# Last node stage of a two-layer graph network: batch norm, elu and residual with feature columns on the partitions

## The chip, the cores and the metric

The kernel runs on one core of a Trainium2 chip. The metric is device time in microseconds of one launch; lower is better. One profiled execution of the kernel before stands beside three timed runs.

## The reference, cut to what matters

There are N = 6250 nodes with D = 256 features, and E = 100000 edges sorted by destination. The first layer is a typed graph attention layer; the second is a graph attention layer with 4 heads of 64 columns. Each layer is preceded by a layer norm and a relu and followed by a residual. Only the end of the second layer is touched by the change:

```python
out = jax.ops.segment_sum(msg, dst, num_segments=n)   # softmax-weighted messages, per node and head
h = out.reshape(n, H * C) + bias
mu = jnp.mean(h, axis=0)                              # over the 6250 nodes, one per column
var = jnp.var(h, axis=0)
h = (h - mu) * jax.lax.rsqrt(var + BN_EPS) * gamma + beta
h = jax.nn.elu(h)
return feature + h                                    # and the outer residual: x + that
```

The mean and the variance run over the nodes, so three passes over the nodes are needed: one that builds h, one that sums squared differences, one that scales.

## The kernel before, in words

The kernel has several stages one after another: sorting of edges, the typed projections, the two edge loops (each a long software pipeline of gathers, matmuls and accumulations), and between and behind them stages over nodes. Each stage with a data-dependent tail ends with branches that all engines take, so nothing of the last stage starts before the edge loop ahead of it has ended.

The last stage (L1797 to L1872) holds nodes on the partitions. A block is 127 nodes on partitions 1 to 127 (partition 0 carries nothing real), and there are NB = 50 blocks, the last of 27 nodes. `acc1` holds for each block, head and node the 64 weighted sums, the denominator and the weight of the node's own message (its self loop). `xw_d` in DRAM holds the projected features (260 numbers per node), `r_d` what the residual adds (256 per node).

Its steps, which the prediction calls A to E:

- Step A, build. Per block two loads (`load_rows`, L173: 112 and 15 rows), then four VectorE operations of 256 columns: own features times own weight (L1832), plus accumulated messages (L1833), times reciprocal denominator (L1834), plus bias (L1835), into `hg`, which keeps all blocks in SBUF. A matmul with a mask of real rows (L1836) adds each block into `sum_ps`.
- Step B, the mean: one ScalarE copy from PSUM (L1838).
- Step C, variance. In ten groups of five blocks: VectorE subtracts the mean in place (L1842), ScalarE squares (L1844), TensorE sums over the rows with five masked matmuls (L1847).
- Step D, scale: Sqrt on ScalarE (L1849), reciprocal and product with gamma on VectorE, on tiles of 128x256 (L1850, L1851).
- Step E, normalise, elu, residual. In ten groups: VectorE multiplies by the scale (L1861), adds beta (L1862), takes the minimum with 0 (L1864), ScalarE takes Exp (L1865), VectorE subtracts 1 (L1866), takes the maximum and adds (L1867), and adds the residual (L1868) that was loaded from `r_d` into one of two buffers (L1858, L1860). The result is stored (L1870, L1872).

All loads and stores of the stage are issued by SyncE in order, through one hardware queue. The order on each engine is set by a scheduler that interleaves the written loops; each engine then works its list strictly in order. TensorE's matmuls of f32 operands show as two weight loads and two matmuls each in the trace, its transposes as one of each.

Two earlier lines serve the prediction as rows to measure by: L410, a VectorE operation with two inputs in SBUF, and L441, a GpSimd multiply of 64x384 with one broadcast input, which runs beside it early in the kernel. L1409 and L1385 are GpSimd additions of 128x256 in the node stage of the first layer, L490 a GpSimd copy of 128x1024, L325 ScalarE operations of 128x896 that also give a sum along the row, L1407 a ScalarE operation with a bias and a scale per partition.

Of the kernel before, what the change touches and what calls it, by code (L numbers as in the profile page):

```python
# [24 lines left out]
def kernel(  # L25
# [1771 lines left out]
    with ExitStack() as st:  # L1797
        cst = st.enter_context(tc.tile_pool(name="e1c", bufs=1))
        wk = st.enter_context(tc.tile_pool(name="e1w", bufs=3))
        pp = st.enter_context(tc.tile_pool(name="e1p", bufs=1, space=PSUM))  # L1800
        rowc = cst.tile([P, 3, D], F32, name="rowc")
        for i, a in enumerate((g_bias, gamma, beta)):
            nc.scalar.dma_start(rowc[:, i, :], bcast(a, D))
        GB = 5
        assert NB % GB == 0
        XB = 4
        xbuf = cst.tile([P, XB, H * XW], F32, name="xbuf")
        nc.gpsimd.memset(xbuf, 0.0)

        real = cst.tile([P, 2, P], F32, name="real")  # L1810
        for i, n in enumerate((BN, LAST)):
            inside = cst.tile([P, 2], F32, name="inside%d" % i)
            nc.vector.tensor_scalar(inside[:, 0:1], ipart, 1.0, None, op0=OP.is_ge)
            nc.vector.tensor_scalar(inside[:, 1:2], ipart, float(n), None, op0=OP.is_le)
            nc.vector.tensor_scalar(real[:, i, :], ones, inside[:, 0:1], inside[:, 1:2], op0=OP.mult, op1=OP.mult)
        xbuf = xbuf.rearrange("p x (h e) -> p x h e", h=H)
        hg = cst.tile([P, NB, D], F32, name="hg")
        es = cst.tile([P, NB, H], F32, name="es")
        den = cst.tile([P, NB, H], F32, name="den")
        for o, i in ((den, DK), (es, DK + 1)):  # L1820
            nc.vector.tensor_tensor(
                o, acc1[:, :, :, i], nhas[:, :, None].to_broadcast([P, NB, H]), op=OP.add
            )
        nc.vector.reciprocal(den, den)
        rbuf = cst.tile([P, 2, GB, D], F32, name="rbuf")
        nc.gpsimd.memset(rbuf, 0.0)
        sum_ps = pp.tile([P, D], F32, name="sum_ps")
        for b in range(NB):
            xs = xbuf[:, b % XB]
            load_rows(xs.rearrange("p h e -> p (h e)"), xw_d, b)  # L1830
            xw = wk.tile([P, H, DK], F32, name="xw")
            nc.vector.tensor_tensor(xw, xs[:, :, :DK], es[:, b, :, None].to_broadcast([P, H, DK]), op=OP.mult)  # L1832
            nc.vector.tensor_add(xw, xw, acc1[:, b, :, :DK])  # L1833
            nc.vector.tensor_tensor(xw, xw, den[:, b, :, None].to_broadcast([P, H, DK]), op=OP.mult)  # L1834
            nc.vector.tensor_add(hg[:, b, :], xw.rearrange("p h e -> p (h e)"), rowc[:, 0, :])  # L1835
            nc.tensor.matmul(sum_ps, real[:, b == NB - 1, :], hg[:, b, :], start=(b == 0), stop=(b == NB - 1))  # L1836
        mu = cst.tile([P, D], F32, name="mu")
        nc.scalar.activation(mu, sum_ps, AF.Copy, scale=1.0 / N)  # L1838
        var_ps = pp.tile([P, D], F32, name="var_ps")
        for g in range(NB // GB):  # L1840
            d = hg[:, g * GB : (g + 1) * GB, :]
            nc.vector.tensor_tensor(d, d, mu[:, None, :].to_broadcast([P, GB, D]), op=OP.subtract)  # L1842
            sq = wk.tile([P, GB, D], F32, name="sq")
            nc.scalar.activation(sq, d, AF.Square)  # L1844
            for i in range(GB):
                b = g * GB + i
                nc.tensor.matmul(var_ps, real[:, b == NB - 1, :], sq[:, i, :], start=(b == 0), stop=(b == NB - 1))  # L1847
        sc = cst.tile([P, D], F32, name="sc")
        nc.scalar.activation(sc, var_ps, AF.Sqrt, bias=eps_t, scale=1.0 / N)  # L1849
        nc.vector.reciprocal(sc, sc)  # L1850
        nc.vector.tensor_mul(sc, sc, rowc[:, 1, :])  # L1851
        for g in range(NB // GB):
            d = hg[:, g * GB : (g + 1) * GB, :]
            r = rbuf[:, g % 2]
            full = GB if (g + 1) * GB < NB else GB - 1
            some = slice(g * GB * BN, (g * GB + full) * BN)
            for o, e in pieces(BN):
                nc.sync.dma_start(r[o + 1 : e + 1, :full, :], by_block(r_d, some)[o:e])  # L1858
            if full < GB:
# [4 lines left out]
            nc.vector.tensor_scalar(ng, d, 0.0, None, op0=OP.min)  # L1864
            nc.scalar.activation(ng, ng, AF.Exp)  # L1865
            nc.vector.tensor_scalar(ng, ng, -1.0, None, op0=OP.add)  # L1866
            nc.vector.scalar_tensor_tensor(ng, d, 0.0, ng, op0=OP.max, op1=OP.add)  # L1867
# [37 lines left out]
```

## Time and profile before

| what | us |
|---|---|
| median of three runs | 3491.12 |
| lowest, highest | 3474.59, 3492.3 |
| profiled execution, its own time | 3487.8 |
| its span, first to last instruction | 3486.0 |
| last stage in it, 3299.4 to 3486.0 | 186.6 |

Over the whole span VectorE is busy 72%, TensorE 67%, GpSimd 60%, ScalarE 54%. The page's rows give busy time, the mean duration of one instruction in ns, and behind the bar the idle time of the engine ahead of those instructions with what ended it. Durations of neighbours on one engine overlap a little, so a run of equal instructions takes somewhat less than their count times the mean. A share averaged over the whole span says nothing on the last stage; that has to be read from windows of it.

### The profile page before, as it was taken

What the parts mean: (1) busy time and instruction counts of PE and PEld (TensorE: products, weight loads), DVE (VectorE), ACT (ScalarE), POOL (GpSimd) and SP (SyncE); (2) the same over time, 40 slices, a digit from 0 to 9 for tenths busy, and PEclk for the clock granted to TensorE, in tenths of its full rate; (3) what the DMA queues carried; (4) which work ended last, traced back from release to release, by engine and by line L of the source; (5) the groups of instructions that cost most, each with busy time, mean ns of one, the idle gap of its engine ahead of it and who ended that gap; (6) DMA issues with size and microseconds to landing.
All of it is one profiled execution on the core that took longest, in us unless ns stands there. A gap on an engine that the chain in (4) does not pass through costs nothing. (4 is left out here: it accounts for less than half of the span.)

```text
span 3486.0 us, 45931 instructions
## 1 busy us (share of the span) xinstructions
PE 2321.6 (67%) x9879; PEld 1626.8 (47%) x9879; DVE 2501.3 (72%) x5600; ACT 1884.6 (54%) x7331; POOL 2105.7 (60%) x2144
## 2 busy tenths in 40 slices
PE   3888765787777777777767772465555556556680
PEld 2555543555555555555536662344344334434440
DVE  8998705898898988889858884455555555555688
ACT  5665561776677777677764441444444444444511
POOL 4665555676666666666614444777777777777300
PEclk9899887998899999999989995677877877777855
DMA  3555687676666767666626663444444444444224
GB/s 99 232 210 219 205 273 222 202 215 198 196 193 199 210 204 206 193 199 207 197 76 171 178 177 103 127 126 129 126 123 127 125 123 128 125 125 127 56 77 132
DMA packets 263729, 571.80 MB, mean 164 GB/s; under 512 B 66395, under 2 KB 162193, under 8 KB 257194
## 3 DMA queue, kind: packets, MB, share of 16 engines
q0 software_dynamic: 124368, 444.93, 41.9%
q1 hardware_dynamic: 131838, 116.55, 12.3%
q10 hardware_dynamic: 7238, 7.22, 0.8%
q8 instruction: 94, 1.54, 0.2%
q14 instruction: 191, 1.56, 0.1%
HBM read 458.42 MB, written 114.06 MB: 164 GB/s over the span
## 5 line engine op out<-in xcount | busy, mean ns | idle before, releaser
L971 POOL DMA_INDIRECT ring<-kv_d,idx x832 | 820.3, 986 | 438.4 <-ACT wrows L1230 184.7
L971 POOL DMA_INDIRECT rows<-xw_d,idx x832 | 873.2, 1049 | 260.8 <-issue 203.8
L1230 ACT ACTIVATE wrows<-ring,wt 128x64 f32<-128x64 f32 x3328 | 834.2, 335 | 0.1
L1713 PE MATMUL aps<-wrows,ebn 128*128 128x264 f32 x1664 | 605.1, 505 | 301.9 <-DVE ebn L1689 151.4
L1074 PE MATMUL qe<-QA,nbe 128*128 x1664 | 467.6, 415 | 170.7 <-DVE nbe L1059 102.5
L1295 PE MATMUL aps<-wrows,ebn 128*128 128x258 f32 x1664 | 520.4, 422 | 38.9 <-ACT wrows L1230 31.7
L1713 PEld LDWEIGHTS aps<-wrows,ebn 128*128 128x128 f32 x1664 | 350.3, 237 | 383.5 <-ACT wrows L1675 332.9
L1074 PEld LDWEIGHTS qe<-QA,nbe 128*128 128x128 f32 x1664 | 330.5, 207 | 265.4 <-issue 165.6
L1675 ACT ACTIVATE wrows<-rows,ex 128x64 f32<-128x64 f32 x1664 | 434.2, 336 | 0.0
L1295 PEld LDWEIGHTS aps<-wrows,ebn 128*128 128x128 f32 x1664 | 318.2, 206 | 131.3 <-ACT wrows L1230 80.7
L1086 DVE TENSOR_TENSOR pr<-ring,qe 128x512 f32<-128x512 f32 x416 | 277.3, 679 | 133.1 <-PE qe L1074 65.8
L1532 ACT COPY asr<-rows 128x16 f32<-128x16 f32 x208 | 44.8, 216 | 575.1 <-DMA rows<-xw_d,idx 575.1
L1729 DVE TENSOR_TENSOR acc<-acc,aps 128x264 f32 x416 | 176.8, 425 | 192.2 <-PE aps L1713 178.0
L1089 DVE TENSOR_REDUCE att<-pr 128x8 f32<-128x512 f32 x416 | 268.7, 677 | 0.1
L1239 DVE SCALAR_TENSOR_TENSOR QA<-QA,same,aps 128x258 f32 x416 | 194.1, 467 | 43.3 <-PE aps L1295 39.4
L578 ACT COPY QA<-rps 128x768 f32<-128x768 f32 x204 | 163.8, 803 | 88.2 <-PE rps L577 85.2
L1577 DVE TENSOR_TENSOR e<-asr,ad 128x128 f32<-128x128 f32 x26 | 10.1, 388 | 215.1 <-ACT asr L1532 215.1
L1390 PE MATMUL nps<-wa_s,tm 128*128 128x256 f32 x600 | 146.6, 397 | 9.2 <-DMA norm<-norm_d,kind_at 6.4
L447 POOL DMA_INDIRECT kv_d<-QA,to_row x51 | 56.7, 1112 | 148.1 <-ACT QA L578 141.5
L1553 PEld LDWEIGHTS <-near 128*128 128x128 bf16 x832 | 96.8, 118 | 102.1 <-issue 41.9
L1689 DVE TENSOR_TENSOR ebn<-ifree,dl 128x512 f32<-128x512 f32 x208 | 142.7, 686 | 0.0
L1208 DVE TENSOR_TENSOR ebn<-ifree,dl 128x512 f32<-128x512 f32 x208 | 140.7, 676 | 2.8 <-PE aps L1295 2.8
(438 smaller groups left out, 3947.3 us busy)
## 6 DMA issues: line engine op xcount, KB each, us to landing
near<-row_d SPq DMA_DIRECT2D x208, 128.0 KB
near<-row_d SPq DMA_DIRECT2D x52, 512.0 KB
ring<-kv_d,idx POOLq DMA_INDIRECT x832
rows<-xw_d,idx POOLq DMA_INDIRECT x832
keeps<-prev_d SPq DMA_DIRECT2D x416, 16.0 KB
xw_d<-xw SPq DMA_DIRECT2D x49, 113.8 KB
xbuf<-xw_d SPq DMA_DIRECT2D x49, 113.8 KB
xbuf<-in_x_dram SPq DMA_DIRECT2D x49, 112.0 KB
```

The lines of the kernel that those rows point to most:

```text
L578: nc.scalar.copy(rel[:, :, i, 2 * c : 2 * c + 2, :].rearrange("p r h e -> p h r e"), ps)
L971: nc.gpsimd.indirect_dma_start(out=to, out_offset=None, in_=table[:, :], in_offset=bass.IndirectOffsetOnAxis(ap=index, axis=0))
L1074: nc.tensor.matmul(qe[:, i, :], oh[j // GT][:, j % GT + i, :], QA[:, 1:, :D][:, bass.ds(bs[j // 2], 1), :].rearrange("p a d -> p (a d)"), ...
L1086: nc.vector.tensor_tensor(pr.rearrange("p t h e -> p t (h e)"), ring[:, lane : lane + 2, slot(t), :], qe, op=OP.mult)
L1089: nc.vector.tensor_reduce(att[:, :, k + j : k + j + 2].rearrange("p h t -> p t h"), pr, AX.X, OP.add)
L1230: nc.scalar.activation(wv[:, j % GT, cols], v[:, cols], AF.Copy, scale=w[:, h, j : j + 1])
L1239: nc.vector.scalar_tensor_tensor(a, a, same[:, t : t + 1], sums.pop(j), op0=OP.mult, op1=OP.add),
L1295: nc.tensor.matmul(sums[j - j % 2], hot[j // GT][:, j % GT, :], wvs[j // GT][:, j % GT, :], start=(j % 2 == 0), stop=(j % 2 == 1),)
L1390: nc.tensor.matmul(tr, m[:, t, c, :], wa_s[:, t, c, :], start=(t == 0 and c == 0), stop=(t == T - 1 and c == FC - 1),)
L1675: nc.scalar.activation(wv[:, part, h, :DK], rows[:, part, h, :DK], AF.Copy, scale=ex[:, 0, h, g * GT + part : g * GT + part + 1],)
L1713: nc.tensor.matmul(sums[t - t % 2], oh[:, t % GT, :], wv[:, t % GT].rearrange("p h e -> p (h e)"), start=(t % 2 == 0), stop=(t % 2 == 1),)
L1729: nc.vector.tensor_tensor(a, a, sums.pop(t).rearrange("p (h e) -> p h e", h=H), op=OP.add)
```

## The change

The stage is rewritten with columns on the partitions (2 chunks of 128) and nodes along the free dimension. Blocks are taken four at a time (13 groups, the last of two). The multiply by the own weight moves to GpSimd; the two remaining VectorE operations work on 1024 columns. TensorE then turns each block by a matmul with the identity (8 per group, the real 127 columns of the identity only), and ScalarE copies the result from PSUM into `hT`, adding the bias as a per-partition scalar and giving the row's sum for the mean. The mean is subtracted in ten VectorE operations of 1250 nodes; the squares with their sums are taken by ScalarE in eight operations and by VectorE in two. Scale and mean are now tiles of 128x2. In the last pass, over tiles of 512 nodes, ScalarE takes Exp and Relu of scale * x + beta, VectorE forms min(exp, 1) + relu, TensorE turns it back by transposes, and VectorE adds the residual and -1 from PSUM. Loads and stores of the last pass are one of 512 KB each per tile, with three buffers; the masks, the buffer clearing and the 15-row pieces of that pass go away. On SyncE's list the first two residual loads stand ahead of the first `xw_d` load, the third behind the last of them; the other loads and stores alternate in the last pass.

The diff, cut to its core:

```diff
     with ExitStack() as st:
         cst = st.enter_context(tc.tile_pool(name="e1c", bufs=1))
         wk = st.enter_context(tc.tile_pool(name="e1w", bufs=3))
-        pp = st.enter_context(tc.tile_pool(name="e1p", bufs=1, space=PSUM))
-        rowc = cst.tile([P, 3, D], F32, name="rowc")
-        for i, a in enumerate((g_bias, gamma, beta)):
-            nc.scalar.dma_start(rowc[:, i, :], bcast(a, D))
-        GB = 5
-        assert NB % GB == 0
-        XB = 4
-        xbuf = cst.tile([P, XB, H * XW], F32, name="xbuf")
-        nc.gpsimd.memset(xbuf, 0.0)
-
...
-        xbuf = xbuf.rearrange("p x (h e) -> p x h e", h=H)
-        hg = cst.tile([P, NB, D], F32, name="hg")
+        pp = st.enter_context(tc.tile_pool(name="e1p", bufs=2, space=PSUM))
+
+        GB = 4
+        XB = 3
+        groups = [(b, min(GB, NB - b)) for b in range(0, NB, GB)]
+        assert GB * BN <= 512
+        xbuf = cst.tile([P, XB, GB, H, XW], F32, name="xbuf")
+        nc.gpsimd.memset(xbuf.rearrange("p x b h e -> p (x b h e)"), 0.0)
         es = cst.tile([P, NB, H], F32, name="es")
         den = cst.tile([P, NB, H], F32, name="den")
-        for o, i in ((den, DK), (es, DK + 1)):
+        for o, i in ((es, DK + 1), (den, DK)):
             nc.vector.tensor_tensor(
                 o, acc1[:, :, :, i], nhas[:, :, None].to_broadcast([P, NB, H]), op=OP.add
             )
         nc.vector.reciprocal(den, den)
-        rbuf = cst.tile([P, 2, GB, D], F32, name="rbuf")
-        nc.gpsimd.memset(rbuf, 0.0)
-        sum_ps = pp.tile([P, D], F32, name="sum_ps")
-        for b in range(NB):
-            xs = xbuf[:, b % XB]
-            load_rows(xs.rearrange("p h e -> p (h e)"), xw_d, b)
-            xw = wk.tile([P, H, DK], F32, name="xw")
-            nc.vector.tensor_tensor(xw, xs[:, :, :DK], es[:, b, :, None].to_broadcast([P, H, DK]), op=OP.mult)
-            nc.vector.tensor_add(xw, xw, acc1[:, b, :, :DK])
-            nc.vector.tensor_tensor(xw, xw, den[:, b, :, None].to_broadcast([P, H, DK]), op=OP.mult)
-            nc.vector.tensor_add(hg[:, b, :], xw.rearrange("p h e -> p (h e)"), rowc[:, 0, :])
-            nc.tensor.matmul(sum_ps, real[:, b == NB - 1, :], hg[:, b, :], start=(b == 0), stop=(b == NB - 1))
-        mu = cst.tile([P, D], F32, name="mu")
-        nc.scalar.activation(mu, sum_ps, AF.Copy, scale=1.0 / N)
-        var_ps = pp.tile([P, D], F32, name="var_ps")
-        for g in range(NB // GB):
-            d = hg[:, g * GB : (g + 1) * GB, :]
-            nc.vector.tensor_tensor(d, d, mu[:, None, :].to_broadcast([P, GB, D]), op=OP.subtract)
-            sq = wk.tile([P, GB, D], F32, name="sq")
-            nc.scalar.activation(sq, d, AF.Square)
-            for i in range(GB):
-                b = g * GB + i
-                nc.tensor.matmul(var_ps, real[:, b == NB - 1, :], sq[:, i, :], start=(b == 0), stop=(b == NB - 1))
-        sc = cst.tile([P, D], F32, name="sc")
-        nc.scalar.activation(sc, var_ps, AF.Sqrt, bias=eps_t, scale=1.0 / N)
+
+        colc = cst.tile([P, 3, FC], F32, name="colc")
+        for i, a in enumerate((g_bias, gamma, beta)):
+            nc.scalar.dma_start(colc[:, i, :], bass.AP(tensor=a.tensor, offset=a.offset, ap=[[1, P], [P, FC]]))
+        hT = cst.tile([P, FC, N], F32, name="hT")
+        sums = cst.tile([P, FC, len(groups)], F32, name="sums")
+        for g, (b, n) in enumerate(groups):
+            xs = xbuf[:, g % XB]
+            full = n if b + n < NB else n - 1
+            for o, e in pieces(BN):
+                nc.sync.dma_start(
+                    xs[o + 1 : e + 1, :full].rearrange("p b h e -> p b (h e)"),
+                    by_block(xw_d, slice(b * BN, (b + full) * BN))[o:e],
+                )
+            if full < n:
+                nc.sync.dma_start(
+                    xs[1 : LAST + 1, full].rearrange("p h e -> p (h e)"), xw_d[(NB - 1) * BN :, :]
+                )
+            xw = wk.tile([P, GB, H, DK], F32, name="xw")
+            xv = xw[:, :n]
+            nc.gpsimd.tensor_tensor(
+                xv, xs[:, :n, :, :DK], es[:, b : b + n, :, None].to_broadcast([P, n, H, DK]), op=OP.mult
+            )
+            nc.vector.tensor_tensor(xv, xv, acc1[:, b : b + n, :, :DK], op=OP.add)
+            nc.vector.tensor_tensor(xv, xv, den[:, b : b + n, :, None].to_broadcast([P, n, H, DK]), op=OP.mult)
+            ps = pp.tile([P, FC, 512], F32, name="xps")
+            w = 0
+            for i in range(n):
+                m = rows_of(b + i)
+                for c in range(FC):
+                    nc.tensor.matmul(
+                        ps[:, c, w : w + m],
+                        xw[:, i].rearrange("p h e -> p (h e)")[:, c * P : (c + 1) * P],
+                        ident[:, 1 : m + 1],
+                        start=True,
+                        stop=True,
+                    )
+                w += m
+            for c in range(FC):
+                nc.scalar.activation(
+                    hT[:, c, b * BN : b * BN + w],
+                    ps[:, c, :w],
+                    AF.Identity,
+                    bias=colc[:, 0, c : c + 1],
+                    accum_out=sums[:, c, g : g + 1],
+                )
+        mu = cst.tile([P, FC], F32, name="mu")
+        nc.vector.tensor_reduce(mu, sums, axis=AX.X, op=OP.add)
+        nc.vector.tensor_scalar(mu, mu, 1.0 / N, None, op0=OP.mult)
+
+        PC = 5
+        PW = N // PC
+        assert PC * PW == N
+        sqs = cst.tile([P, FC, PC], F32, name="sqs")
+        for k in range(PC):
+            for c in range(FC):
+                d = hT[:, c, k * PW : (k + 1) * PW]
+                nc.vector.tensor_scalar(d, d, mu[:, c : c + 1], None, op0=OP.subtract)
+        for k in range(PC):
+            for c in range(FC):
+                d = hT[:, c, k * PW : (k + 1) * PW]
+                if k == PC - 1:
+                    sq = cst.tile([P, PW], F32, name="sqv")
+                    nc.vector.scalar_tensor_tensor(
+                        sq, d, 1.0, d, op0=OP.mult, op1=OP.mult, accum_out=sqs[:, c, k : k + 1]
+                    )
+                else:
+                    sq = cst.tile([P, PW], F32, name="sqa")
+                    nc.scalar.activation(sq, d, AF.Square, accum_out=sqs[:, c, k : k + 1])
+        sc = cst.tile([P, FC], F32, name="sc")
+        nc.vector.tensor_reduce(sc, sqs, axis=AX.X, op=OP.add)
+        nc.scalar.activation(sc, sc, AF.Sqrt, bias=eps_t, scale=1.0 / N)
         nc.vector.reciprocal(sc, sc)
-        nc.vector.tensor_mul(sc, sc, rowc[:, 1, :])
-        for g in range(NB // GB):
-            d = hg[:, g * GB : (g + 1) * GB, :]
-            r = rbuf[:, g % 2]
-            full = GB if (g + 1) * GB < NB else GB - 1
-            some = slice(g * GB * BN, (g * GB + full) * BN)
-            for o, e in pieces(BN):
-                nc.sync.dma_start(r[o + 1 : e + 1, :full, :], by_block(r_d, some)[o:e])
-            if full < GB:
-                nc.sync.dma_start(r[1 : LAST + 1, full, :], r_d[(NB - 1) * BN :, :])
-            nc.vector.tensor_tensor(d, d, sc[:, None, :].to_broadcast([P, GB, D]), op=OP.mult)
-            nc.vector.tensor_tensor(d, d, rowc[:, 2:3, :].to_broadcast([P, GB, D]), op=OP.add)
-            ng = wk.tile([P, GB, D], F32, name="sq")
-            nc.vector.tensor_scalar(ng, d, 0.0, None, op0=OP.min)
-            nc.scalar.activation(ng, ng, AF.Exp)
-            nc.vector.tensor_scalar(ng, ng, -1.0, None, op0=OP.add)
-            nc.vector.scalar_tensor_tensor(ng, d, 0.0, ng, op0=OP.max, op1=OP.add)
-            nc.vector.tensor_add(ng, ng, r)
-            for o, e in pieces(BN):
-                nc.sync.dma_start(by_block(out, some)[o:e], ng[o + 1 : e + 1, :full, :])
-            if full < GB:
-                nc.sync.dma_start(out[(NB - 1) * BN :, :], ng[1 : LAST + 1, full, :])
+        nc.vector.tensor_mul(sc, sc, colc[:, 1, :])
+
+        GN = 4
+        for o in range(0, N, GN * P):
+            w = min(GN * P, N - o)
+            r = wk.tile([P, GN, D], F32, name="r")
+            whole = w // P
+            rest = w - whole * P
+            if whole:
+                nc.sync.dma_start(r[:, :whole, :], r_d[o : o + whole * P, :].rearrange("(b p) d -> p b d", p=P))
+            if rest:
+                nc.sync.dma_start(r[:rest, whole, :], r_d[o + whole * P : o + w, :])
+            low = wk.tile([P, FC, GN * P], F32, name="low")
+            high = wk.tile([P, FC, GN * P], F32, name="high")
+            for t, f in ((low, AF.Exp), (high, AF.Relu)):
+                for c in range(FC):
+                    nc.scalar.activation(
+                        t[:, c, :w], hT[:, c, o : o + w], f, bias=colc[:, 2, c : c + 1], scale=sc[:, c : c + 1]
+                    )
+            nc.vector.scalar_tensor_tensor(
+                low[:, :, :w], low[:, :, :w], 1.0, high[:, :, :w], op0=OP.min, op1=OP.add
+            )
+            y = wk.tile([P, GN, D], F32, name="y")
+            for i in range(0, GN, 2):
+                some = [j for j in (i, i + 1) if j * P < w]
+                if not some:
+                    continue
+                ps = pp.tile([P, 2, D], F32, name="yps")
+                for j in some:
+                    m = min(P, w - j * P)
+                    for c in range(FC):
+                        nc.tensor.transpose(
+                            ps[:m, j - i, c * P : (c + 1) * P], low[:, c, j * P : j * P + m], ident
+                        )
+                k = len(some)
+                m = min(P, w - i * P)
+                nc.vector.scalar_tensor_tensor(
+                    y[:m, i : i + k, :], ps[:m, :k, :], -1.0, r[:m, i : i + k, :], op0=OP.add, op1=OP.add
+                )
+            if whole:
+                nc.sync.dma_start(out[o : o + whole * P, :].rearrange("(b p) d -> p b d", p=P), y[:, :whole, :])
+            if rest:
+                nc.sync.dma_start(out[o + whole * P : o + w, :], y[:rest, whole, :])
```

More of the change, by code (lines that the diff above doesn't have):

```diff
@@ L1799 @@
         wk = st.enter_context(tc.tile_pool(name="e1w", bufs=3))
-        pp = st.enter_context(tc.tile_pool(name="e1p", bufs=1, space=PSUM))
-        rowc = cst.tile([P, 3, D], F32, name="rowc")
-        for i, a in enumerate((g_bias, gamma, beta)):
-            nc.scalar.dma_start(rowc[:, i, :], bcast(a, D))
-        GB = 5
-        assert NB % GB == 0
-        XB = 4
-        xbuf = cst.tile([P, XB, H * XW], F32, name="xbuf")
-        nc.gpsimd.memset(xbuf, 0.0)
[L1810 to L1815, printed above, removed]
-        xbuf = xbuf.rearrange("p x (h e) -> p x h e", h=H)
-        hg = cst.tile([P, NB, D], F32, name="hg")
+        pp = st.enter_context(tc.tile_pool(name="e1p", bufs=2, space=PSUM))
[5 more added lines that the diff above has]
+        nc.gpsimd.memset(xbuf.rearrange("p x b h e -> p (x b h e)"), 0.0)
         es = cst.tile([P, NB, H], F32, name="es")
         den = cst.tile([P, NB, H], F32, name="den")
-        for o, i in ((den, DK), (es, DK + 1)):
+        for o, i in ((es, DK + 1), (den, DK)):
             nc.vector.tensor_tensor(
```

## The prediction

> **What bounds the kernel now.** I read the chain that ended last first. It holds only the last stage, because the branches ahead of it cut everything off: the stage is a stretch in series with the rest, 3299.4 to 3486.0 us, and its gains and losses go into the time one for one. Then the windows of the stage by step (columns: stretch, its length, busy us and count per engine, TensorE's granted clock, DMA share, GB/s):
>
> ```profile
> 3305.00:3371.00 66.00, 53.12 (x96) 24.06 (x96) 65.93 (x197) 0.00 (x0) 0.00 (x0) 0.50 0.43 112
> ...
> 3377.00:3402.00 25.00, 24.43 (x100) 20.79 (x100) 11.34 (x9) 13.19 (x12) 0.00 (x0) 0.89 0.00 1
> 3402.00:3470.00 68.00, 0.00 (x0) 0.00 (x0) 67.74 (x58) 12.64 (x11) 0.00 (x0) 0.53 0.44 125
> ```
>
> VectorE (third pair) fills steps A and E; TensorE fills step C. ScalarE and GpSimd are nearly idle. The groups of the stage give the prices:
>
> ```profile
> L1834 DVE TENSOR_TENSOR xw<-xw,den 128x256 f32<-128x256 f32 x50 | 20.4, 407 | 0.1
> L1847 PE MATMUL var_ps<-sq,real 128*128 128x256 f32 x100 | 24.4, 411 | 3.3 <-ACT sq L1844 3.3
> L1867 DVE SCALAR_TENSOR_TENSOR sq<-hg,sq 128x1280 f32<-128x1280 f32 x10 | 14.8, 1485 | 0.1
> L1864 DVE TENSOR_SCALAR sq<-hg 128x1280 f32<-128x1280 f32 x10 | 8.1, 819 | 0.1
> L1844 ACT ACTIVATE sq<-hg 128x1280 f32<-128x1280 f32 x10 | 12.7, 1270 | 9.5 <-PE var_ps L1847 7.7 <-DVE hg L1842 1.6
> L1826 POOL MEMSET rbuf<- 128x2560 f32 x1 | 2.2, 2227 | 0.0
> ```
>
> Step A is 50 x 4 VectorE operations at 0.335 each (67 us; 407 ns overlap a little). Step C is 100 matmuls in 24.4. Step E is ten groups of four operations of 1.40 and two of 0.74, with 1.28 of table load or wait here and there: 3404.3 to 3480.7, then 5.3 for the last stores.
>
> The new row that matters is a GpSimd multiply beside VectorE. The trace has it early, L441 beside L410, both in the timeline (start, us, engine):
>
> ```profile
> 21.54 3.37 DVE L410 TENSOR_TENSOR QA<-ifree,prow_f 128x896 bf16<-128x896 f32 x2
> ...
> 26.49 2.08 DVE L410 TENSOR_TENSOR QA<-ifree,prow_f 128x896 bf16<-128x896 f32 x2
> ...
> 20.66 4.95 POOL L441 TENSOR_TENSOR ra_s<-ra_s,pri 64x384 f32<-64x384 f32 x3 [1.72 <-DMA ra_s<-in_L_gnn_rel_att_dram]
> ```
>
> While the three GpSimd multiplies run, a L410 starts every 1.65 us instead of every 1.0, and each multiply also lasts 1.65: they take turns. So 0.65 us of it is GpSimd's own, and a two-input VectorE operation and a GpSimd multiply add up instead of overlapping.
>
> **Step A, build.** Start: the memset grows from 1040 to 3120 columns, 2.23 x 3120/2560 = 2.7, so the first `xw_d` load is issued at 3302.2. The two residual loads (0.52 MB each) stand ahead of it on SyncE's queue. The best stretch of step E moves
>
> ```profile
> 3420.00:3430.00 10.00, 0.00 (x0) 0.00 (x0) 10.00 (x10) 2.54 (x2) 0.00 (x0) 0.50 0.90 250
> ```
>
> 250 GB/s at a share of 0.90; I take 270 (bounds 250 and 278). So 1.05 MB take 3.9 and the first group of 0.52 MB 1.9: it lands near 3308, where before the first block was there at 3304.8.
>
> Per group, VectorE does two operations of 1024 columns. L1867 has 1.40 per start at 1280 columns; the slope (1485 - 407)/1024 is 1.05 ns per column, so 1.13 each, 2.26. The GpSimd multiply of 1024 columns is not in the trace. Bounds: L441's own 0.65 for 384 columns, scaled, gives 1.75; L1409's 0.72 for 256, scaled with its fixed part, 2.9. L441 has the same broadcast input but only 64 partitions, L1409 all 128; I take 2.1, nearer L441. With the lock a group costs 2.1 + 2.26 + 0.1 for the wait of the second operation on the first = 4.45, and 12.5 groups 55.6. All else lies beside it. TensorE: 8 matmuls of two halves; at clock 0.50 a weight load is 0.25 apart in step A now, so 4.0 per group, a cover of only 0.45. ScalarE: L325 with its sum read starts every 1.17 for 896 columns (30 in 33.9 us); 508 columns at 0.84 ns less per column (L1844 against the 411 ns of L1645's 256) are 0.84, two 1.7. Loads: 1.9.
>
> So VectorE ends near 3363.6, the last groups drain through TensorE and ScalarE in 4 (weight loads as above), and step B's reduction costs 0.5: the mean is there at 3368.1, before at 3374.2. Gain 6.1. With 1.75 it is 10.5, with 2.9 a loss of 4.
>
> On the multiply the Trainium skill speaks against the change: "GPSIMD Engine Reference", Engine selection, would have no ordinary elementwise work on GpSimd, and its Performance versus the Vector engine measures 4497 ns for 2048 columns. An estimate from that page is 2.3 for 1024, which would make the group 4.65 and the sum 2.5 us later.
>
> **Step C, variance.** Ten subtractions of 1250 columns cost 0.74 each, the start distance of L1864; the first ends after 0.8. Then ScalarE's eight squares with sums, 1.17 + 354 x 0.84 ns = 1.47 each, 11.7. VectorE's two squares end at 7.4 + 2 x 1.45 = 10.3, inside. Total 12.5; before, 3374.2 to 3401.6 = 27.3. Gain 14.8. The 24.4 of masked matmuls are gone, and ScalarE is what is late next.
>
> **Step D, scale.** The Sqrt table load now follows the last square (1.28), Sqrt 0.3 (L158 has 295 ns), then the Exp table load 1.28, with reciprocal and product of two columns beside it: 3.0. Before 2.75. Loss 0.25; ScalarE's last pass starts near 3383.8. The second load cost nothing before, as VectorE worked meanwhile.
>
> **Step E.** Per tile of 512 nodes: ScalarE four operations; L1407 (bias and scale per partition) has 600 ns for 256, plus 256 x 0.84, less the overlap of 0.09 that neighbours show: 0.73, so 2.9. VectorE: one of 1024 (1.13) and two of 512 from PSUM, L1396's 467 ns for 256 plus 0.27, so 2.6 in all. TensorE: eight transposes of 0.29 (L197), 2.3. Transfers: 0.52 MB in, 0.52 out, 3.9 at 270 GB/s. The transfers are the dearest, so they set the pace. Three residual loads are done ahead of the stage; 6.4 + 6.4 - 1.6 = 11.2 MB remain and take 41.5 (40.3 to 45). The first result is ready after 2.9 + 1.1 + 2.3 + 0.7 = 7.0. Behind each load on SyncE's list stands a store that waits for VectorE (once three in a row ahead of three loads); who waits for that is VectorE's residual add, and ScalarE three tiles on. I add 1.5 for such holes (0 to 6), and 2.2 for the last landing. Sum 52.2, end 3436.0; before 3404.3 to 3486.0, 81.7. Gain 29.5.
>
> A page bears on this too: "DMA: Bandwidth & Descriptors", Specifications, gives line rate from 512 B per descriptor and 358 GB/s from HBM. With that the transfers would be an estimated 31 us and ScalarE's 35 would set step E, about 6 us shorter; the trace's rows of 1 KB do not reach it.
>
> Sum: 6.1 + 14.8 - 0.25 + 29.5 = 50 us, span 3436, time 3438 against the profiled execution's 3487.8. That execution lies 3.3 below the median of the runs shown and 13 above their lowest, so a median can lie some way off for no reason of the change. 0.5% is 17 us, about what a measurement of this kernel can tell from no change.
>
> **Rivals.** (1) The multiply is as dear as L441's lines look, 1.65 for 384 columns, 4.4 for 1024, and still locked: 6.75 per group, 29 us more, 3467. For: strided input, broadcast; against: that 1.0 of the 1.65 is VectorE's turn. 0.12. (2) No lock in this form: TensorE's 4.0 or, with a clock near the 0.89 of step C, 3.3 per group sets step A: 5 to 14 less, 3424 to 3432. For: L1409 keeps 721 to 725 ns beside mostly one-input work; against: the lines above. 0.10. (3) Step E keeps the 125 GB/s of its window now, by waiting stores on SyncE: 11.2 MB take 90, 48 more, 3486, no change. Against: VectorE paced that window, and three buffers instead of two. 0.08. (4) Slower: the GpSimd multiply over the four-dimensional broadcast pattern costs over 7.5 us (7.4 ns per column), under the lock. From there 12.5 groups of 9.9 eat all 50 and 17 more; at 10 us the time is 3537. For: a 24-column GpSimd operation, L438, shows 1106 ns; against: most of that is a wait for VectorE's operation beside it, and no row has over 2.9 ns per column after its wait. 0.05. My forecast has 0.65.
>
> **Numbers.** Range: low from rival 2's 3424 with the spread of the runs below their median, 3412; high is rival 1, 3467, with the 3.3 by which the median of the runs shown lies above the profiled execution, 3470. Outside lie rivals 3 and 4 and a little of the rest, 0.18. Faster: forecast, 1 and 2, 0.87; same: rival 3, 0.08; slower 0.05.
>
> **What would show it.** Right: in step A, L1835 near 2 us of its own and VectorE's starts pushed by it; TensorE's matmuls in the shade; step C's ScalarE squares end to end at 1.47; in step E a DMA share near 1 and VectorE waiting for `r`. Wrong: a step A over 75 us with GpSimd busy throughout; step E with the DMA share near 0.5 and SyncE waiting; TensorE's clock at 0.50 with weight loads end to end in step A would mean that it, not the lock, is the bound.

## The result, and the profile after

The changed kernel takes 3435.0 us (median of four runs, 3433.0 to 3436.3) against 3491.7 for the kernel before (median of four). The ratio is 0.985, with a 95% interval of 0.983 to 0.987. The profiled execution took 3434.3 us; its span is 3432.4, and the stage lies in it from 3300.5 to the end.

The windows of the stage in the kernel after (columns: stretch, its length, busy us and count of PE, PEld, DVE, ACT and POOL, TensorE's granted clock, DMA share, GB/s):

```profile
3300.00:3309.00 9.00, 0.00 (x0) 0.00 (x0) 2.37 (x3) 0.00 (x0) 2.70 (x1) 0.55 0.79 219
3309.20:3360.60 51.40, 28.17 (x176) 27.56 (x177) 43.59 (x26) 14.42 (x40) 31.10 (x13) 0.73 0.45 119
3368.00:3383.00 15.00, 0.00 (x0) 0.00 (x0) 9.38 (x15) 14.72 (x22) 0.00 (x0) 0.54 0.00 1
3390.00:3400.00 10.00, 5.96 (x26) 4.62 (x24) 8.11 (x10) 9.79 (x15) 0.00 (x0) 0.51 0.86 281
3410.00:3420.00 10.00, 5.51 (x27) 4.36 (x28) 8.07 (x11) 7.26 (x12) 0.00 (x0) 0.65 0.99 333
3420.00:3433.00 13.00, 1.31 (x9) 0.63 (x7) 2.10 (x5) 0.00 (x0) 0.00 (x0) 0.64 0.43 145
```

The second line is step A. VectorE shows 43.6 busy us and GpSimd 31.1 of 51.4: more than the whole together, and neither is full. The third line is mostly steps C and D, where TensorE does nothing any more and ScalarE is full. The last two are the second half of step E: a DMA share of 0.99, and then 13 us in which hardly anything computes.

Some groups of the stage (line, engine, operation, tiles and shapes, count | busy us, mean ns | idle before them, and what ended it):

```profile
L1845 PE MATMUL xps<-ident,xw 128*128 128x127 f32 x196 | 31.5, 337 | 35.5 <-DVE xw L1839 35.5
L1835 POOL TENSOR_TENSOR xw<-xbuf,es 128x1024 f32<-128x1024 f32 x12 | 29.1, 2442 | 21.7 <-PE xps L1845 15.4 <-DMA xbuf<-xw_d 6.0
L1839 DVE TENSOR_TENSOR xw<-xw,den 128x1024 f32<-128x1024 f32 x12 | 21.7, 1811 | 0.4
L1838 DVE TENSOR_TENSOR xw<-xw,acc 128x1024 f32<-128x1024 f32 x12 | 21.4, 1780 | 12.8 <-POOL xw L1835 12.8
L1907 DVE SCALAR_TENSOR_TENSOR low<-low,high 128x1024 f32<-128x1024 f32 x12 | 14.4, 1218 | 4.7 <-ACT high L1904 4.7
L1883 ACT ACTIVATE sqa<-hT 128x1250 f32<-128x1250 f32 x8 | 10.0, 1246 | 1.6 <-DVE hT L1872 1.4
```

L1838, L1839 and L1907 are three VectorE operations of 1024 columns with two inputs. L1907 has a mean of 1218 ns, the other two 1800: those run beside GpSimd's L1835, whose mean is 2442 ns. The timeline of the first round of step A shows what the means hide (start, us, engine, operation):

```profile
3309.29 1.90 POOL L1835 TENSOR_TENSOR xw<-xbuf,es 128x1024 f32<-128x1024 f32 x1 [6.05 <-DMA xbuf<-xw_d]
3311.15 1.90 POOL L1835 TENSOR_TENSOR xw<-xbuf,es 128x1024 f32<-128x1024 f32 x1
3313.16 2.72 POOL L1835 TENSOR_TENSOR xw<-xbuf,es 128x1024 f32<-128x1024 f32 x1
3311.22 2.90 DVE L1838 TENSOR_TENSOR xw<-xw,acc 128x1024 f32<-128x1024 f32 x1 [7.38 <-POOL xw L1835]
3314.16 2.81 DVE L1839 TENSOR_TENSOR xw<-xw,den 128x1024 f32<-128x1024 f32 x1
3316.89 1.21 DVE L1838 TENSOR_TENSOR xw<-xw,acc 128x1024 f32<-128x1024 f32 x1
...
3321.01 2.51 POOL L1835 TENSOR_TENSOR xw<-xbuf,es 128x1024 f32<-128x1024 f32 x1 [5.12 <-PE xps L1845]
```

GpSimd multiplies three groups, and each VectorE operation beside it lasts 2.8 to 2.9. The second multiply has a VectorE operation beside it and lasts 1.90, as long as the first, which has none: it isn't slowed, and VectorE's L1838 stands until it is done. The third lasts 2.72, as it stands for L1838 first. Then GpSimd waits 5 us for a free `xw`, and VectorE's operations are back at 1.2. A round of three groups takes 11.7 to 12.3 us.

### The profile page after: what moved, and what is told of

Same layout as the page of the kernel before. It is cut to its first block, busy times and chain, and to the rows that moved or that the text cites. A ratio compares the mean times of both kernels' runs of the same rounds, so it can differ in the third digit from the quotient of the medians.

```text
span 3432.4 us, 45921 instructions
## 1 busy us (share of the span) xinstructions
PE 2286.5 (67%) x9977; PEld 1621.8 (47%) x9977; DVE 2431.4 (71%) x5405; ACT 1924.1 (56%) x7430; POOL 2138.1 (62%) x2156
## 5 line engine op out<-in xcount | busy, mean ns | idle before, releaser
L1713 PE MATMUL aps<-wrows,ebn 128*128 128x264 f32 x1664 | 590.3, 495 | 318.4 <-DVE ebn L1689 164.5
L1074 PE MATMUL qe<-QA,nbe 128*128 x1664 | 475.2, 420 | 172.2 <-DVE nbe L1059 99.9
L1713 PEld LDWEIGHTS aps<-wrows,ebn 128*128 128x128 f32 x1664 | 343.5, 233 | 398.8 <-ACT wrows L1675 348.3
L1295 PEld LDWEIGHTS aps<-wrows,ebn 128*128 128x128 f32 x1664 | 317.0, 205 | 132.4 <-ACT wrows L1230 80.2
L1682 DVE TENSOR_TENSOR wrows<-rows,ex 128x512 f32<-128x512 f32 x208 | 142.0, 683 | 0.4
```

Source lines behind the costliest of these rows:

```text
L1074: nc.tensor.matmul(qe[:, i, :], oh[j // GT][:, j % GT + i, :], QA[:, 1:, :D][:, bass.ds(bs[j // 2], 1), :].rearrange("p a d -> p (a d)"), ...
L1295: nc.tensor.matmul(sums[j - j % 2], hot[j // GT][:, j % GT, :], wvs[j // GT][:, j % GT, :], start=(j % 2 == 0), stop=(j % 2 == 1),)
L1713: nc.tensor.matmul(sums[t - t % 2], oh[:, t % GT, :], wv[:, t % GT].rearrange("p h e -> p (h e)"), start=(t % 2 == 0), stop=(t % 2 == 1),)
```

## The experiments

The part ahead of the stage is the same in every kernel, but in the profiled executions of the first eight the stage begins anywhere between 3299 and 3319 us. Steps that an edit leaves alone repeat within 0.4 us (only step A of e2 is 1.2 off). So each edit is read from its step; all lengths below come from the timelines of the profiled executions, in us. "Start" is from the memset of the load buffers to the first multiply, A from there to the first use of the mean, C from there until ScalarE turns to the square root (its table load included), D until the first operation of the last pass, E the rest, and the stage is the sum.

| kernel | start | A | C | D | E | stage |
|---|---|---|---|---|---|---|
| before | 5.4 | 69.4 | 27.3 | 2.8 | 81.7 | 186.6 |
| after | 8.8 | 56.9 | 11.9 | 2.9 | 51.5 | 131.9 |
| e1_mult_on_vector | 9.0 | 47.3 | 11.9 | 2.9 | 51.1 | 122.2 |
| e2_residual_early | 7.2 | 55.6 | 11.9 | 2.9 | 50.8 | 128.4 |
| e3_both | 7.2 | 47.3 | 11.9 | 2.9 | 50.7 | 120.0 |
| e5_order_in_e | 8.9 | 56.6 | 11.9 | 2.9 | 45.6 | 125.9 |
| e6_both_and_order | 7.4 | 47.3 | 11.9 | 2.9 | 45.6 | 115.1 |
| e7_tail_pieces | 7.1 | 47.3 | 11.9 | 2.9 | 48.3 | 117.5 |
| e8_all | 7.1 | 47.3 | 11.9 | 2.9 | 43.1 | 112.3 |
| e9_more_buffers | 8.7 | 55.0 | 11.9 | 2.9 | 51.7 | 130.2 |
| e10_variance_split | 5.7 | 47.4 | 7.5 | 2.9 | 43.5 | 107.0 |

**Step A: turns, overlap or buffers.** The theory was that a GpSimd multiply and a two-input VectorE operation never run at the same moment. The first test gives the multiply back to VectorE:

```diff
-            nc.gpsimd.tensor_tensor(
+            nc.vector.tensor_tensor(
                 xv, xs[:, :n, :, :DK], es[:, b : b + n, :, None].to_broadcast([P, n, H, DK]), op=OP.mult
...
```

> The kernel after, with one edit in step A: the multiply by a node's own weights (L1835) runs on VectorE instead of GpSimd. Theory (exclusive turns: a two-input VectorE operation and a GpSimd multiply never run at the same moment, so step A is the sum of both engines' work): a group becomes three VectorE operations of 1.13 = 3.4 us instead of 1.9 + 2 x 1.13, the 12.5 groups 42.5 against 51.4 measured, the time 9 us lower, near 3426; TensorE's 31.5 busy us then become the next late work and may keep 2 of the 9. Rival (the engines overlap for the most part and GpSimd takes a third of the work off VectorE): VectorE's load rises by half, step A is as long or up to 14 us longer, 3435 to 3449.

Step A fell from 56.9 to 47.3, by 9.6; the ratio to the kernel before is 0.981 (0.979 to 0.983). The groups of e1:

```profile
L1839 DVE TENSOR_TENSOR xw<-xw,den 128x1024 f32<-128x1024 f32 x12 | 14.7, 1225 | 0.1
L1838 DVE TENSOR_TENSOR xw<-xw,acc 128x1024 f32<-128x1024 f32 x12 | 14.7, 1225 | 0.1
L1835 DVE TENSOR_TENSOR xw<-xbuf,es 128x1024 f32<-128x1024 f32 x12 | 14.7, 1222 | 5.7 <-DMA xbuf<-xw_d 5.7
```

All three operations now take 1.22 us. VectorE has half as much work again and step A is shorter, so the idle GpSimd was no help: a multiply there keeps VectorE waiting longer than VectorE needs to do it. TensorE kept none of the gain.

The second test puts the same operation on GpSimd in the kernel before:

```diff
-            nc.vector.tensor_tensor(xw, xs[:, :, :DK], es[:, b, :, None].to_broadcast([P, H, DK]), op=OP.mult)
+            nc.gpsimd.tensor_tensor(xw, xs[:, :, :DK], es[:, b, :, None].to_broadcast([P, H, DK]), op=OP.mult)
```

> The kernel before, with one edit in its step A: of the four VectorE operations per block of 125 nodes the multiply by the own weights (L1832, 256 columns) runs on GpSimd. Theory (exclusive turns): a block costs 0.72 on GpSimd (the row of L1409, 256 columns) plus 3 x 0.335 on VectorE = 1.73 instead of 1.34, 50 blocks 19 us more, near 3507 for the profiled execution. Rival (the engines overlap): VectorE's four operations become three, 17 us less, near 3471.

The ratio is 1.0019 (1.0000 to 1.0038). From the memset to the mean it takes 79.0 us (3305.6 to 3384.6), 4.2 more than before. That is neither 19 more nor 17 less. The timeline of e4, first of GpSimd and then of VectorE within one block, shows why:

```profile
3322.79 0.73 POOL L1832 TENSOR_TENSOR xw<-xbuf,es 128x256 f32<-128x256 f32 x1 [0.70 <-DVE hg L1835]
3324.21 0.72 POOL L1832 TENSOR_TENSOR xw<-xbuf,es 128x256 f32<-128x256 f32 x1 [0.70 <-DVE hg L1835]
```

```profile
3322.63 0.41 DVE L1834 TENSOR_TENSOR xw<-xw,den 128x256 f32<-128x256 f32 x1
3322.97 0.83 DVE L1833 TENSOR_TENSOR xw<-xw,acc 128x256 f32<-128x256 f32 x1
3323.72 0.41 DVE L1835 TENSOR_TENSOR hg<-xw,rowc 128x256 f32<-128x256 f32 x1
```

A block starts every 1.42 us. L1833 lasts 0.83 instead of 0.41: it stands 0.42 for GpSimd. GpSimd's record of 0.73 begins 0.18 before VectorE's L1834 makes room at 3322.97, and ends 0.13 after VectorE has gone on. So of its 0.73 only 0.42 is a turn. That 0.42 + 3 x 0.335 gives the 1.42 again is no further evidence, as the 0.42 was read from the same rows; but the 0.65 that the prediction read from L441 for 384 columns, scaled to 256, is 0.43. The turns are shown; what was wrong in the expectation was the price, as the row's duration is more than the turn.

The third test keeps the multiply on GpSimd and gives `xw` more buffers:

```diff
-            xw = wk.tile([P, GB, H, DK], F32, name="xw")
+            xw = wk.tile([P, GB, H, DK], F32, name="xw", bufs=5)
```

> The kernel after, with the multiply on GpSimd as it is, but five instead of three buffers for the tile xw of step A (to make room, step E has two instead of three of high and of y; only step A is read here). In the kernel after GpSimd waits 15.4 us in step A for TensorE to give a xw buffer back. Theory (exclusive turns: step A is the sum of GpSimd's 1.9 and VectorE's 2 x 1.13 per group, and GpSimd's wait is only where its turn is over): step A, from the first multiply to the mean, stays at 56.8 within 1.5; GpSimd's waits for buffers shrink, and the waits inside VectorE's operations grow instead. Rival (the three buffers bound it, the engines would overlap if they had more): GpSimd's 1.9 hides behind VectorE's work, step A falls towards 12.5 x 2.3 + 5 = 34, or 40 with TensorE's 31.5 busy us as the limit.

e9 and e10 ran on a chip on which all that comes ahead of the stage takes some 540 us longer, for the kernel before too; the stage itself doesn't, so it is compared by its steps. Step A is 55.0, 1.9 shorter and just past the margin given. The groups of e9:

```profile
L1835 POOL TENSOR_TENSOR xw<-xbuf,es 128x1024 f32<-128x1024 f32 x12 | 30.9, 2590 | 14.5 <-PE xps L1845 7.3 <-DMA xbuf<-xw_d 6.0 <-DVE xw L1838 1.2
L1838 DVE TENSOR_TENSOR xw<-xw,acc 128x1024 f32<-128x1024 f32 x12 | 24.9, 2071 | 7.4 <-POOL xw L1835 7.4
L1839 DVE TENSOR_TENSOR xw<-xw,den 128x1024 f32<-128x1024 f32 x12 | 23.3, 1944 | 0.4
```

GpSimd's waits for TensorE halve, from 15.4 to 7.3, and VectorE's operations grow from 1.78 and 1.81 to 2.07 and 1.94. The wait moved, as the turns say. Three buffers were not the bound, or for 1.9 us at most.

**Step E: the residual loads.** In the kernel after, VectorE waits 7.4 us for residual tiles, 5.1 of it for the last two:

```profile
3422.74 1.29 DVE L1924 SCALAR_TENSOR_TENSOR y<-yps,r 128x512 f32<-128x512 f32 x2 [2.35 <-DMA r<-r_d]
3426.74 0.42 DVE L1924 SCALAR_TENSOR_TENSOR y<-yps,r 106x256 f32<-106x256 f32 x1 [2.71 <-DMA r<-r_d]
```

The obvious suspect was that these loads are issued behind stores that wait. e2 reads all of them early, into memory that step A has used up:

```diff
+        spare = acc1.rearrange("p b h e -> p (b h e)")
...
-            r = wk.tile([P, GN, D], F32, name="r")
+            r = spare[:, o // P * D : (o + w + P - 1) // P * D].rearrange("p (g d) -> p g d", d=D)
```

> The kernel after, with one edit in step E: the residual tiles are read into the memory of the messages acc1, which step A has used up, so all residual loads are issued behind the last load of step A and run beside steps A's end, C and D; in step E only the stores move. Two residual loads that stood ahead of the first load of step A go too. Theory (residual loads that queue behind waiting stores make the tail of step E, in which ScalarE has been done for 14.5 us): E goes from 51.5 to about 41 (ScalarE's 37, and 4 for the last tile and its store), step A's first load lands 1 to 2 us earlier, together 10 to 12 less, near 3424. Rival (the volume that has to be moved, or ScalarE, sets E and the wait for the residual only stands beside it): within 2 us of 3435.

The ratio to before is 0.983 (0.980 to 0.986), not to be told from the kernel after. The start is 1.5 shorter, as expected; step E is 50.8, 0.7 shorter where 10 were expected. The theory fell as it stood, but the edit did not act alone: VectorE's list came out of the scheduler in another order. What follows ScalarE's last instruction of the stage fell from 14.5 to 11.1 us, and that instruction ended 2.7 later, 39.7 into step E instead of 37.0. The waits of step E in e2 (waiting line, what it waited for: us in all, times, longest):

```profile
PE yps L1920 <- DVE low L1908: 36.4, 10, 20.9
...
DVE y L1925 <- PE yps L1920: 10.3, 19, 1.3
```

The 7.4 us for the residual are gone, and those for TensorE have grown from 4.8 to 10.3. VectorE's timeline shows the order behind it:

```profile
3403.97 1.21 DVE L1908 SCALAR_TENSOR_TENSOR low<-low,high 128x1024 f32<-128x1024 f32 x1
3406.46 0.69 DVE L1925 SCALAR_TENSOR_TENSOR y<-yps,acc 128x512 f32<-128x512 f32 x1 [1.27 <-PE yps L1920]
3407.31 0.69 DVE L1925 SCALAR_TENSOR_TENSOR y<-yps,acc 128x512 f32<-128x512 f32 x1 [0.16 <-PE yps L1920]
3407.92 1.22 DVE L1908 SCALAR_TENSOR_TENSOR low<-low,high 128x1024 f32<-128x1024 f32 x1
```

VectorE sums the elu of a tile (L1908), then stands in front of TensorE's transposes of that same tile until it may add the residual; the next tile's sum, whose inputs ScalarE has ready, is queued behind. The engines take turns, and such a tile takes 3.95. Not every tile is one: from the second sum to the twelfth a tile takes 3.38 in e2, and 3.07 in the kernel after, which has the same pattern in its first tiles and lets the sums run ahead from the eighth on.

> Both edits together: the multiply of step A on VectorE, and the residual tiles read early into the memory of the messages. Theory (two separate stages in series, A by turns and E by its residual loads): the gains add, 19 to 21 us less than 3435, near 3415. If one is hidden by the other (the residual loads are issued later because step A's loads come sooner, and collide with them), 12 to 17 less, 3418 to 3423. Rivals of both edits together: 3435 to 3449.

e3 (ratio 0.983, 0.980 to 0.986) has A as in e1 and the start and E as in e2, each within 0.1: the steps add up, and nothing collides. The stage is 11.9 shorter; 19 to 21 were expected, since E's part did not come.

e5 and e6 write the order of step E out, e5 on the kernel after, e6 on e3:

```diff
...
+        with tc.manual_schedule():
+            lows = [elu(*tiles[0])]
+            for t in range(len(tiles)):
+                if t + 1 < len(tiles):
+                    lows.append(elu(*tiles[t + 1]))
+                back(*tiles[t], lows[t], rs[t])
```

Here `elu` is ScalarE's exp and relu with VectorE's sum, and `back` the transposes, the residual addition and the store of one tile; e5 loads `rs[t + 3]` behind `back` of tile t.

> The kernel after, with one edit in step E: its program order is written out, so that VectorE does the elu sum (L1907) of tile t+1 ahead of the two residual additions of tile t, and SyncE loads residual tile t+3 behind the store of tile t. In the trace of e2_residual_early the waits for the residual were gone and step E still took 50.8 us: VectorE stood 1.27 in front of TensorE's transposes of a tile, with the next tile's elu sum queued behind, so that the two engines took turns, 1.23 + 1.96 + 0.76 = 3.95 per tile against ScalarE's 3.0. Theory (two limits, this order and the residual loads behind waiting stores, each hidden behind the other): the order alone gains part, E from 51.5 to 46 to 50. Rival 1 (the order alone is the limit, the loads are not): E near 44.5, 7 less. Rival 2 (the loads alone are): E stays at 51.5 within 1.

> e3_both with the same written order in step E (elu sum of tile t+1 ahead of the residual additions of tile t). Theory (with the residual early and the order mended ScalarE is the limit): E from 50.7 to ScalarE's 37.4, 1.5 for the last short tile and 5.3 for its store = 44, the stage from its memset to the end from 120.0 to 113, the time 6 to 7 below e3_both, near 3422. Rival (TensorE, at a clock of 0.50, or the stores set E): E stays at 49 to 51.

Step E is 45.6 in both: just under the 46 to 50 of e5's theory, 1.1 over its rival 1 and 1.6 over the 44 of e6. Reading the residual early adds nothing once the order is written. e6 differs from e3 in that order alone, with no load left in step E, so the 5.1 from 50.7 to 45.6 is what the turns cost there. e5 says less, since it writes SyncE's list too, one load behind each store. In the kernel after three stores came in a row and three loads behind them. The first two lines are SyncE's list, the others the residual loads in the chain that ended last:

```profile
3401.51 5.45 SPq L1928 DMA_DIRECT2D out_dram<-y  x3
3407.06 2.06 SPq L1897 DMA_DIRECT2D r<-r_d  x3
...
3399.33 5.82 DMA r<-r_d
3407.06 4.75 DMA r<-r_d
3420.55 6.07 DMA r<-r_d
```

These loads are 16.6 us of the chain. So in the kernel after the turns hold up the first tiles, and loads that stand behind stores hold up later ones; the theory of two limits is not refuted. e5 mends both lists at once and has 0.8 us of waits for the residual left; a kernel with VectorE's order mended alone was not run, so the share of each is not shown. The ratio of e5 is 0.983 (0.980 to 0.987) and that of e6 0.978 (0.976 to 0.981). VectorE in e6:

```profile
3401.77 1.23 DVE L1912 SCALAR_TENSOR_TENSOR low<-low,high 128x1024 f32<-128x1024 f32 x1 [0.40 <-ACT high L1909]
3402.91 1.28 DVE L1934 SCALAR_TENSOR_TENSOR y<-yps,acc 128x512 f32<-128x512 f32 x2
3404.60 1.23 DVE L1912 SCALAR_TENSOR_TENSOR low<-low,high 128x1024 f32<-128x1024 f32 x1 [0.40 <-ACT high L1909]
```

A tile now takes 2.83, and VectorE waits for ScalarE alone. ScalarE works without a gap for 35.4 of the 45.6 us, in e5 too. In e5 the windows of this stretch show what the transfers can do when nothing holds them back, residual loads and stores together:

```profile
3420.00:3430.00 10.00, 6.47 (x28) 5.09 (x27) 8.80 (x12) 10.00 (x15) 0.00 (x0) 0.50 1.07 372
```

**Step E: the last 106 rows.** e2's windows, first a stretch with residual loads of 512 KB, then one in which only the last store, of 106 rows, is under way:

```profile
3350.00:3360.00 10.00, 7.20 (x51) 7.04 (x49) 7.49 (x6) 3.21 (x9) 2.48 (x2) 0.83 1.09 385
3424.00:3426.00 2.00, 0.00 (x0) 0.00 (x0) 0.00 (x0) 0.00 (x0) 0.00 (x0) 0.50 0.13 45
```

e7 splits the load and the store of these rows:

```diff
...
-            if rest:
-                nc.sync.dma_start(out[o + whole * P : o + w, :], y[:rest, whole, :])
+            for lo, hi in pieces(rest):
+                nc.sync.dma_start(out[o + whole * P + lo : o + whole * P + hi, :], y[lo:hi, whole, :])
```

> e3_both with the residual load and the store of the last 106 nodes each split into 96 and 10 rows. In e2_residual_early's trace those last 106 KB move at 45 GB/s, 2.4 us, while a tile of 512 KB moves at some 380. Theory (the piece of 106 rows goes out one row after the other): with 96 rows the last store lands about 2 us earlier, E from 50.7 to 48.7. Rival (the last store is a fixed time from issue to landing): no change, or 0.3 more for the second issue.

Step E fell from 50.7 to 48.3, by 2.4 where 2 were expected; the ratio, 0.981 (0.979 to 0.984), is too coarse for it. A share of 0.13 is two of 16 engines. The Trainium skill ("DMA: Bandwidth & Descriptors", section "Why a DMA increments its semaphore by 16 and not by 1") says that a transfer is spread over the largest number of engines up to 16 that divides its outermost size. For 106 rows that is 2 and for 96 it is 16: the measured 45 against 385 GB/s agrees.

> All edits together: the multiply of step A on VectorE, the residual early, the written order in step E, the last 106 rows in two pieces. Theory: the gains of separate steps add, 7 + 2 on top of e3_both: E 42, the stage from its memset to the end 111 against 131.9 in the kernel after, the time 20 below it, near 3415 to 3420. Rival (the last store's landing stays): E 44, 2 us more.

e8 has all edits: step E 43.1 (between the expected 42 and the rival's 44), the stage 112.3 against 131.9. Its ratio is 0.978 (0.976 to 0.980), 0.7% below that of the kernel after; its median is 3428, where 3415 to 3420 was expected, on a chip where the kernel before takes 3501. The gain of E over e6 is again 2.5.

**Step C.** e10 leaves ScalarE five squares instead of eight, and lets the first load wait for a third of the memset only:

```diff
-                nc.vector.tensor_scalar(d, d, mu[:, c : c + 1], None, op0=OP.subtract)
+            nc.scalar.activation(
+                sq, hT[:, 0, k * PW : (k + 1) * PW], AF.Square, bias=less[:, 0:1], accum_out=sqs[:, 0, k : k + 1]
+            )
...
+            nc.vector.scalar_tensor_tensor(
+                sv, d, mu[:, 1:2], d, op0=OP.subtract, op1=OP.mult, accum_out=sqs[:, 1, k : k + 1]
+            )
...
-        nc.gpsimd.memset(xbuf.rearrange("p x b h e -> p (x b h e)"), 0.0)
+        for x in range(XB):
+            nc.gpsimd.memset(xbuf[:, x].rearrange("p b h e -> p (b h e)"), 0.0)
```

> e8_all with two more edits, each in a step of its own. Step C: no subtraction of the mean; ScalarE squares the first 128 columns with the mean as its bias (five squares instead of eight), VectorE forms (h - mean) x h of the other 128 with its sum (five, instead of ten subtractions and two squares), and step E's exp and relu get the bias beta - mean x scale. Stage start: the memset of the three load buffers is three instructions, so that the first load waits for the first alone. Theory (ScalarE's squares in series, one every 1.37, set step C; VectorE's work stands beside them): C from 11.9 to 5 x 1.37 + 0.5 = 7.4, D stays at 2.9; memset to first multiply from 7.1 to 5.3; the stage from 112.3 to 106, the time 6 below e8_all, near 3421. Rival for C (VectorE's five products of 1250 columns with their sums, 1.46 each, are the longer side and must wait for the mean of both halves): 7.8 to 8.5. Rival for the start (the load's own time from issue to landing hides the memset): no change there.

Step C is 7.5 (expected 7.4) and D is unchanged. Eight squares started every 1.37, the first after 1.0; now five start every 1.46, the first after 0.2: 11.9 and 7.5, so it was the series of squares that set C. The start is 5.7 (expected 5.3), the stage 107.0. The ratio to the kernel before is 0.978 (0.974 to 0.982). The two sides of step C end almost together:

```profile
L1879 DVE SCALAR_TENSOR_TENSOR sqv<-hT,mu 128x1250 f32<-128x1250 f32 x5 | 7.6, 1520 | 0.1
L1874 ACT ACTIVATE sqa<-hT,less 128x1250 f32<-128x1250 f32 x5 | 6.7, 1338 | 0.8 <-DVE less L1871 0.7
```

## Why the prediction was right, and where it was not

The time was 3435 where 3438 was predicted, and the stage became 54.7 us shorter where the sum had 50. By its steps:

- **Start of A.** Right: the first group was expected 8.6 us after the memset began and was there after 8.8. The two residual loads that stand ahead of it cost 1.5 of it (e2).
- **The lock.** Right, and shown by e1, e4 and e9. The term for the multiply was a little too dear, 2.1 where the trace has 1.9, and the group came to 4.1 instead of 4.45. The bound of 2.9, scaled from a GpSimd row of 0.72 for 256 columns, was far off: in e4 0.42 of such a row is the turn. The drain behind the last group took 5.5 instead of 4.5. So step A and its start gained 9.2 (12.5 less 3.3) where 6.1 stood in the sum.
- **TensorE in A.** Its "cover of only 0.45" was too small: it was busy 31.5 us in step A, 2.5 per group against the predicted 4.0. Where the clock was 0.50 (3318 to 3321) the weight loads do stand end to end, but 16 of them take 3.0 us, 0.19 each; the 0.25 of the prediction came from matmuls of 256 columns, and these have 127. Over the whole step the clock was 0.73. Such stretches were named as a sign that TensorE is the bound; it was not, as e1 left it the same work and step A fell by 9.6.
- **C.** Right in its mechanism (ScalarE is what is late next; e10), 11.9 against 12.5: the squares start every 1.37, not 1.47.
- **D.** 2.9 against 3.0.
- **E.** The sum held, 51.5 against 52.2, but by luck: the step "The transfers are the dearest, so they set the pace" was wrong, and two terms beside it were too small. The 270 GB/s was scaled from a window in which VectorE was full; loads and stores reach 372 in e5, so 11.2 MB need an estimated 30 us, not 41.5. The order of two lists held E up instead. In the first tiles VectorE's list made it take turns with TensorE, 3.95 a tile where 2.83 will do; the prediction had each engine's sum per tile, but not that a list in which the next tile's work stands behind a wait makes two engines' sums add. Later SyncE's list kept residual loads behind stores, and VectorE waited 7.4 us for them; the prediction had such holes, at 1.5. And "the last landing", put at 2.2, took 5.2 from its issue, some 2.4 of it because 106 rows go out at 45 GB/s (e7). A waiting `r` and a DMA share near 1 were named as signs that the step was right. Both were there (7.4 us, 0.99), but with both lists written (e5) 0.8 us of the waits is left, and the same bytes move through the same queue in a step 5.9 shorter. The other reading in the prediction, transfers of 31 and ScalarE's 35 as the limit, was set aside because the rows of the trace did not reach its rate. With the lists written that is what the runs show: 372 GB/s in e5, and 35.4 us of ScalarE in e5 and e6.
- **Rivals.** (1) and (4), a dear multiply, are out by its 1.90 us. (2), no lock, is out by e1 and e4. (3), step E at 125 GB/s, is out by the windows of step E, 281 and 333.

On the multiply the page cited in the prediction was right to speak against GpSimd: with the multiply on VectorE step A is 9.6 us shorter (e1), though the estimate of 2.3 us was above the 1.90 measured. Another page has the rule for it: "SBUF — State Buffer", section "SBUF: two separate sides", says that a VectorE operation with two SBUF inputs and a GpSimd operation that reads SBUF hold a shared port pair each for its whole instruction. The second multiply of the kernel after, 1.90 like the first while L1838 stands 2.90 beside it, agrees with that.

What the change itself gained is thus made up of 15.4 in C, 30.2 in E, 9.2 in start and A, and 0.1 lost in D. The edits of e10 find 9.5 more in A, 8 in E, 4.4 in C and 3.1 in the start.

## What to carry to other kernels

An idle engine is no free place for work: first look whether its instructions and those of the busy engine ever overlap, and price them by the distance of their starts, since a row's duration may hold a wait. Where two engines hand a tile back and forth, look at what stands behind the waiting instruction in an engine's own list; putting the next tile's work ahead of that wait was worth 5.1 us here (e6 against e3). A long wait for a transfer and a full DMA share do not show that the volume is the limit: change the order of the lists, that of the queue too, and see whether they stay. And where a scheduler makes the order, an edit can change it elsewhere, as in e2: read the order again in each trace.

## What the runs showed of the hardware that was not expected

- A GpSimd multiply and a two-input VectorE operation exclude each other for whole instructions: a multiply of 1024 columns lasts 1.90 with and without a VectorE operation beside it, and that operation lasts 2.90 instead of 1.2.
- Loads in rows of 1 KB reach 385 GB/s at a share of 1.09 (e2), loads and stores together 372 at 1.07 (e5), where the best stretch of step E before showed 250; one transfer of 106 rows reaches 45.
- The steps of the stage repeat within 0.4 us, but for step A of e2, on a chip too where the part ahead of them takes 540 us longer.
